# Weights loaded directly behind x, three small rows on GpSimd's queue, the second y ahead of the scores, and adapters gathered two slots earlier

## The chip, the core and the metric

The kernel runs on one core of a Trainium2 chip. A core has five engines with a queue of instructions each: PE (matrix products; its weight loads are shown apart, as PEld), DVE (vector work), ACT (activation functions and copies), POOL (GpSimd) and SP (which here only issues transfers). Transfers between device memory and the core's on-chip memory run on 16 DMA engines that all queues share; SP, ACT and POOL can each issue them. The engines wait for each other through semaphores. What is measured is the device time of one execution in microseconds (us); lower is better.

## What is computed

Eight batches of 128 tokens with 512 features pass through two residual layers. The first adds a product with one of 16 adapter matrices, chosen by an index per batch. The second adds grouped-query attention over a paged cache of 512 old keys plus the 128 new ones. (The cached rows of the eight batches are found through a table of page numbers.)

```python
def _L0_cond_ref(x, adapter_ids, weight):
    w = weight[adapter_ids]
    return jnp.einsum('bsi,boi->bso', x, w)

def _L1_cond_ref(x, Wq, Wk, Wv, Wo, q_norm_w, k_norm_w, k_cache, v_cache, block_table, cache_seqlens):
    q = jnp.einsum('bsd,ed->bse', x, Wq).reshape(bsz, seqlen, HQ, D)
    k = jnp.einsum('bsd,ed->bse', x, Wk).reshape(bsz, seqlen, HK, D)
    v = jnp.einsum('bsd,ed->bse', x, Wv).reshape(bsz, seqlen, HK, D)
    q = _rmsnorm(q, q_norm_w)
    k = _rmsnorm(k, k_norm_w)
    pos = cache_seqlens[:, None] + jnp.arange(seqlen)[None, :]
    q = _rope(q, pos)
    k = _rope(k, pos)
    kc = k_cache[block_table].reshape(bsz, L, HK, D)
    vc = v_cache[block_table].reshape(bsz, L, HK, D)
    k_all = jnp.concatenate([kc, k], axis=1)
    v_all = jnp.concatenate([vc, v], axis=1)
    ...
    scores = jnp.einsum('bqhd,bkhd->bhqk', q, k_all) * SCALE
    scores = jnp.where(valid[:, None, None, :], scores, -1e+30)
    probs = jax.nn.softmax(scores, axis=-1)
    o = jnp.einsum('bhqk,bkhd->bqhd', probs, v_all)
    o = o.reshape(bsz, seqlen, HQ * D)
    return jnp.einsum('bse,de->bsd', o, Wo)

x = x + _L0_cond_ref(x, itok_B_0_15, L0_cond_weight)
x = x + _L1_cond_ref(x, ..., itok_Bx16_0_63, itok_B_207_1644)
```

There are 32 query heads and 8 key heads of 128 features (`HQ`, `HK`, `D`), and all arithmetic is in 32-bit floating point.

## The kernel before

**Steps and slots.** The 8 key heads are cut into 4 groups of 2. A step `i` is one pair of group `g` and batch `b`; there are 32 steps, and the eight batches of group 0 come first (steps 0 to 7). A step has 8 slots, one for each query head `h`. In a slot PE computes one head's scores (`sc`, L1040), DVE adds the mask and finds the row's bound (L1050), ACT takes the exponential (L1066), POOL divides by the sum (L1114) and DVE transposes blocks of the probabilities (L875). The list `main` holds the remaining matrix work of the step: the products with the values of the step before (`o`), the projections of the next step (`pj_kv`, `pj_q`), the output products (`out`). It is dealt out evenly over the slots by estimated cost. The order in which the program is written is the order in which each engine executes it; nothing is rearranged by a scheduler.

**Queues.** SP issues most transfers, among them the store of transposed probabilities (`xp`), their load back in the other layout (`pT`), and the same pair for the queries (`xq`, `qT`) and for the cached keys (`xk`, `kT`). Transfers of one queue are issued in order, and an issue that waits holds back those behind it. ACT issues the loads of x and of the first weights at the start, and weights of later groups. POOL issues the indirect loads (gathers): cached keys (`kc`), cached values (`vc`) and adapters (`lraw`), each about 1 us of POOL's time.

**The start.** `load_x(0)` puts the first x on ACT's queue (L111), then three short rows (L118, called at L120 to L122): the sequence lengths, the page table and the rope frequencies. Then follow the key weights and the value weights, half a megabyte each (`load_first`, L149). SP loads the first adapter, the query weights, x of batch 1, adapter 1, x of batch 2 and the output weights. POOL fills constants, builds the identity, and issues three other rows: the adapters' numbers and the two norm weights. PE then turns (transposes through PSUM, against the identity) everything that is loaded: `warm` is nine such transposes of the identity itself, with no use but to have PE run. `rope_angles` copies the row to floating point on DVE, spreads it over the 128 partitions by a product on PE (`spread(0)`, L386), and computes angles and their reduction to one turn. `row_numbers` and `row_values` compute on POOL the row numbers by which keys and values are gathered; `row_rest` spreads the second part of the row (`spread(1)`), from which come `lora_ix`, the row numbers of the adapters, and the norm weights `wn`. `rope_sin`, `rope_cos` and `rope_table` make the tables SW and CW that the rotation of k and q reads.

**The adapters.** Batches 0 and 1 have their adapters loaded by SP at the start. For the others `gather_lora(b)` issues one indirect load of 1 MB into the only buffer of that kind. `turn_lora` transposes it in four pieces (`lw`), in slots 0 to 3 of step `b - 2` (2 to 5 of step 0), and `lora_y` multiplies x with it (`y`), after which x + y is transposed again (`turn_x1`). In step `i` below 5, `gather_lora(b + 3)` stands in slot 6, behind the scaling of that slot's probabilities and behind two gathers of values.

**The second y.** Just before step 0, one of the four pieces of `lora_y(1)` is emitted; the other three go into `main` of step 0, behind the first scores, and after them output weights and `turn_x1(1)`. Pieces of work that evacuate PSUM stand in a list `pending`, and `run(pending)` emits them.

**Buffers.** PSUM has four buffers of 512 columns (`ps_mm`) for everything but the scores, and two (`ps_sc`) for scores.

Of the kernel before, what the change touches and what calls it, by code (L numbers as in the profile page):

```python
# [18 lines left out]
P = 128  # L19
# [33 lines left out]
def lora_then_paged_attention(  # L53
# [49 lines left out]
    def load_x(b, eng=None):  # L103
        (eng or nc.sync).dma_start(out=acc[b], in_=x[b])
# [12 lines left out]
    def load_row(eng, to, lo, src):  # L117
        eng.dma_start(out=to[:, lo : lo + src.shape[-1]], in_=src)  # L118

    load_row(nc.scalar, row_i, at_len, seqlens.unsqueeze(0))  # L120
    load_row(nc.scalar, row_i, at_bt, block_table.rearrange("b n -> (b n)").unsqueeze(0))
    load_row(nc.scalar, row_f, 0, inv_freq.unsqueeze(0))  # L122


    def weight_rows(kind, g, n, m=1):
# [72 lines left out]
    nc.gpsimd.memset(ones, 1.0)  # L198
    ident = const.tile([P, P], FP, name="ident")
    make_identity(nc, ident)  # L200
    wn = const.tile([P, 2, D], FP, name="wn")
    par = const.tile([P, 1], I32, name="par")
    nc.gpsimd.iota(par, pattern=[[0, 1]], base=0, channel_multiplier=1)
# [171 lines left out]
    def table_set(func):  # L375

        nc.scalar.activation(rope["one"], rope["one"], func)
# [11 lines left out]
    def rope_angles():  # L389
        nc.vector.tensor_copy(row_f[:, at_len:at_ids], row_i[:, at_len:at_ids])  # L390
        row = spread(0)
        nc.vector.tensor_copy(len_f, row[:, at_len:at_bt])
        nc.vector.tensor_copy(
            rows_of["bt_f"].rearrange("p c q -> p (c q)"), row[:, at_bt:at_ids]
        )
        par_f = rope["par"] = const.tile([P, 1], FP, name="par_f")
        nc.vector.tensor_copy(par_f, par)
        pos = const.tile([P, B], FP, name="pos")
        nc.vector.tensor_scalar(pos, len_f, par_f, None, ALU.add)
        def temp(tag):  # L400
            t = work.tile([P, 4, D], FP, tag=tag, name=f"rope_{tag}")
            return t.rearrange("p h (u d) -> p (h u) d", u=2)

        ang, turns, sin, cos = temp("q0"), temp("q1"), temp("tq0"), temp("sw")
        nc.vector.tensor_tensor(
            ang,
            pos.unsqueeze(2).to_broadcast([P, B, H2]),
            row[:, 0:H2].unsqueeze(1).to_broadcast([P, B, H2]),
            ALU.mult,
        )  # L410
        nc.vector.tensor_scalar(turns, ang, 1.0 / (2 * math.pi), ROUND, ALU.mult, ALU.add)
        nc.vector.tensor_scalar(turns, turns, ROUND, None, ALU.subtract)
        for part in (TWO_PI_1, TWO_PI_2, TWO_PI_3):
            nc.vector.scalar_tensor_tensor(
                out=ang, in0=turns, scalar=-part, in1=ang, op0=ALU.mult, op1=ALU.add
            )
        nc.vector.tensor_scalar(ang, ang, PI_BELOW, -PI_BELOW, ALU.min, ALU.max)
        rope.update(ang=ang, sin=sin, cos=cos)

    def row_rest():  # L420

        nc.vector.tensor_copy(row_f[:, at_ids:at_wn], row_i[:, at_ids:at_wn])
        row = spread(1)
        nc.vector.scalar_tensor_tensor(
            out=lora_ix,
            in0=row[:, 0:B],
            scalar=float(HID // 4),
            in1=rope["par"].to_broadcast([P, B]),
            op0=ALU.mult,
            op1=ALU.add,  # L430
        )
        for n in range(2):
            lo = B + (1 - n) * D
            nc.scalar.copy(wn[:, n, :], row[:, lo : lo + D])
# [493 lines left out]

    on_act, on_vec = nc.scalar.copy, nc.vector.tensor_copy

    t = ps_mm.tile([P, HID], FP, tag="mm", name="warm")
    for n in range(9):
        nc.tensor.transpose(t[:, 0:P], ident, ident)
    row_parts()
    table_set(AF.Sin)
    rope_angles()
    row_numbers()
    for c in range(LC):
        gather_k(0, c)
    row_values()  # L940
    turn_x(0, on_act)
    for n in range(4):
        turn_weights(("kv", 0, n), on_act)
    for j in range(4):
        turn_lora_row(0, j, (on_act, on_vec)[j % 2])
    row_rest()
    rope_sin()
    rope_table(1, ("sin",))
    rope_cos()
# [11 lines left out]
        f()  # L961
    rope_table(0)
    make_mask(0)
    run(pending)
    for _, f in project(0, "q0"):
        f()
# [3 lines left out]
    run(pending)  # L970
    for c in range(LC):
        gather_k(1, c)
    row_tables(range(1, G))
    for _, f in project(0, "q1"):
        f()
    turn_x(1, on_vec)
    for c in range(KC):
        turn_lora(1, c, on_vec if c % 2 else on_act, True)
    gather_lora(2)
    turn_k(0, 0, on_act)  # L980
    turn_q(0, 0, on_act)
    turn_x(2, on_vec)
    y_1 = lora_y(1)
    y_1.pop(0)[1]()
    for _ in range(3):
        load_next()

# [2 lines left out]
    for i, (g, b) in enumerate(steps):  # L990
        s = st[i]
        main = []
        if i == 0:
            main += y_1

            def second(n):
                run(pending)
                turn_weights(("o0", 0, n))
                if n == 2:
                    turn_x1(1)  # L1000

            main += [(4 * TR * (1 + n // 2), lambda n=n: second(n)) for n in range(3)]
            main += [(4 * TR, lambda: turn_weights(("o0", 0, 3)))]
        early = i >= B - 2
        if i and not early:
            main += values(i - 1, 0)
# [22 lines left out]
        for h in range(8):  # L1029
# [98 lines left out]
                    pending.append(lambda i=i: make_mask(i + 1))  # L1128
            if g == 0 and h == 6 and b + 3 < B:
                load_x(b + 3)  # L1130
                gather_lora(b + 3)
            if 8 * i + h - 1 in turn_when:
                load_next()
# [58 lines left out]
```

## Time and profile before

| What | Value |
|---|---|
| Time before, median of 3 runs | 1201.35 us (1200.62 to 1202.08) |
| The profiled execution, its own time | 1202.72 us |
| Its span, first to last instruction | 1201.0 us |
| PE busy | 1183.7 us (99%) |
| DVE busy | 733.3 us (61%) |
| POOL busy | 673.3 us (56%) |
| ACT busy | 530.4 us (44%) |
| Bytes moved | 328.04 MB, mean 273 GB/s |

The span is what the profile's instructions cover; the 1.7 us between it and the execution's own time lie around it. Times in the profile's views count from the start of the span. In a line of a timeline the first number is the start, the second the duration, then engine, line of the code, operation, what is written and read, shapes, and a count; in square brackets stands how long the engine was idle before it, and what ended that. An engine's name with a q is its queue: it issued a transfer there. "Landing" is when a transfer's semaphore says that all has arrived.

A busy share of 99% does not say that PE runs at its full pace: matmuls are pipelined, their ends are modelled, and the same instruction takes twice as long when PE's clock is halved.

### The profile page before, as it was taken

The numbers are of one execution on the slowest core, as the hardware profiler recorded it, in microseconds if no ns is written. First come the engines' busy times: TensorE is split into PE (matmuls) and PEld (weight loads), VectorE is DVE, ScalarE is ACT, GpSimd is POOL, SyncE is SP. The second block draws the span as 40 slices with busy tenths as digits, with TensorE's granted clock in tenths as the row PEclk, the third lists the DMA queues.
The fourth block names the chain that finished last, engine by engine and source line by source line (L and its number), as shares of the span: only waits on it lengthen the run. The fifth ranks groups of instructions, "written<-read, shape, count | busy, mean of one in ns | idle before, by whom it ended". The sixth has DMA issues, their size and how long they took to land.

```text
span 1201.0 us, 12981 instructions
## 1 busy us (share of the span) xinstructions
PE 1183.7 (99%) x3421; PEld 580.3 (48%) x3421; DVE 733.3 (61%) x1676; ACT 530.4 (44%) x1647; POOL 673.3 (56%) x780
## 2 busy tenths in 40 slices
PE   7999999999999999999999999999999999999998
PEld 5555444454444444444444444444444444444454
DVE  5575655656566667666566666666557655565651
ACT  4564444444444444444444444444444444444432
POOL 4466456445565556656655556565555656655540
PEclk9999999999999999999999999999999999999999
DMA  8288788778989989888898998888898987777761
GB/s 289 96 276 270 262 297 275 238 258 259 312 288 301 341 296 305 295 281 291 291 297 287 334 326 285 309 268 305 268 317 282 297 290 257 249 251 247 257 221 60
DMA packets 187120, 328.04 MB, mean 273 GB/s; under 512 B 13094, under 2 KB 106023, under 8 KB 178087
## 3 DMA queue, kind: packets, MB, share of 16 engines
q1 hardware_dynamic: 124000, 238.71, 58.9%
q10 hardware_dynamic: 49798, 48.64, 12.4%
q0 software_dynamic: 13248, 39.86, 10.1%
q8 instruction: 28, 0.46, 0.2%
q14 instruction: 46, 0.37, 0.1%
HBM read 195.04 MB, written 132.12 MB: 272 GB/s over the span
## 4 chain that ended last, share of the span: by engine, by line
PE 90%; DMA 3%; POOL 3%; issue 1%; DVE 1%; ACT 1%; ACTq 0%; POOLq 0%; DVEq 0%
PE sc L1040 22%; PE o L563 21%; PE pj_q L563 17%; PE out L563 16%; PE pj_kv L563 9%; DMA lraw<-in_L_cond_weight_dram,lora_ix 2%; PE y L563 2%; PE lw L478 1%; DMA raw_kv<-in_L_cond_Wv_dram 1%; DMA w_q<-xw_q 1%; POOL kc L614 1%; PE kt L767 1%; POOL p L1114 1%; POOL vc L614 1%; POOL rs L691 0%
## 5 line engine op out<-in xcount | busy, mean ns | idle before, releaser
L1050 DVE CUSTOM_DVE_ANT_0 p<-sc,mask 128x640 f32<-128x640 f32 x256 | 210.9, 824 | 403.4 <-PE sc L1040 403.1
L1066 ACT ACTIVATE p<-p,mn 128x640 f32<-128x640 f32 x256 | 211.6, 827 | 313.9 <-DVE mn L1050 310.2
L1040 PE MATMUL sc<-kT,qT 128*128 128x512 f32 (+1 forms) x1024 | 319.4, 434 | 0.2 <-ACT qT L777 0.2
L1114 POOL TENSOR_SCALAR p<-p,rc 128x640 f32<-128x640 f32 x252 | 201.9, 801 | 186.0 <-DVE rc L1107 184.1
L1040 PEld LDWEIGHTS sc<-kT,qT 128*128 128x128 f32 x1024 | 190.6, 191 | 226.8 <-issue 206.9
L563 PE MATMUL pj_q<-w_q,x1T 128*128 128x512 f32 x512 | 236.1, 593 | 0.3 <-DMA w_q<-xw_q 0.2
L563 PE MATMUL out<-w_o,oT 128*128 128x512 f32 (+1 forms) x528 | 235.0, 580 | 0.9 <-ACT oT L842 0.7
L563 PE MATMUL o<-pT,vc 128*128 128x512 f32 x512 | 235.4, 592 | 0.0
L875 DVE STREAM_TRANSPOSE tp<-p 128x640 f32<-128x640 f32 x252 | 211.0, 837 | 5.7 <-POOL p L1114 5.4
L614 POOL DMA_INDIRECT kc<-in_L_cond_k_cache_dram,key_ix x128 | 131.2, 1025 | 31.8 <-issue 31.5
L614 POOL DMA_INDIRECT vc<-in_L_cond_v_cache_dram,val_ix x128 | 127.9, 999 | 30.5 <-issue 30.3
L696 ACT ACTIVATE q<-q,rs 128x128 f32<-128x128 f32 x256 | 81.9, 390 | 132.5 <-POOL q L683 124.7
L563 PEld LDWEIGHTS out<-w_o,oT 128*128 128x128 f32 x528 | 95.4, 190 | 91.6 <-issue 88.9
L563 PEld LDWEIGHTS pj_q<-w_q,x1T 128*128 128x128 f32 x512 | 92.7, 190 | 94.4 <-issue 92.5
L563 PEld LDWEIGHTS o<-pT,vc 128*128 128x128 f32 x512 | 92.5, 190 | 92.3 <-issue 86.3
L563 PE MATMUL pj_kv<-w_kv,x1T 128*128 128x512 f32 x256 | 116.6, 593 | 0.7 <-ACT x1T L480 0.7
L675 POOL TENSOR_TENSOR k<-sw 128x256 f32<-128x256 f32 x31 | 23.0, 741 | 160.1 <-PE kt L767 139.4
L683 POOL TENSOR_TENSOR q<-q,sw 128x512 f32<-128x512 f32 x59 | 74.4, 1262 | 44.1 <-DVE sw L666 44.0
L650 ACT ACTIVATE sq<-pj_q 128x128 f32<-128x128 f32 x256 | 70.8, 277 | 59.5 <-PE pj_q L563 50.5
L691 POOL TENSOR_TENSOR rs<-ss,mhalf 128x6 f32<-128x6 f32 x64 | 77.1, 1205 | 5.3
L563 PEld LDWEIGHTS pj_kv<-w_kv,x1T 128*128 128x128 f32 x256 | 46.0, 190 | 45.5 <-issue 44.6
L563 PE MATMUL o<-pT,vn 128*128 128x512 f32 x128 | 65.7, 595 | 0.0
(124 smaller groups left out, 879.6 us busy)
## 6 DMA issues: line engine op xcount, KB each, us to landing
xp<-tp SPq DMA_DIRECT2D x63, 1280.0 KB, 6.0
pT<-xp SPq DMA_DIRECT2D x63, 1280.0 KB, 6.6
xk<-tk SPq DMA_DIRECT2D x31, 512.0 KB, 7.6
kT<-xk SPq DMA_DIRECT2D x62, 256.0 KB, 6.5
xq<-tq SPq DMA_DIRECT2D x59, 256.0 KB, 3.8
qT<-xq SPq DMA_DIRECT2D x59, 256.0 KB, 6.0
st_q<-in_L_cond_Wq_dram ACTq DMA_DIRECT2D x24, 256.0 KB, 5.3
xw_q<-tw_q ACTq DMA_DIRECT2D x24, 256.0 KB, 4.6
```

What stands on the lines that cost most here:

```text
L563: nc.tensor.matmul(y[0], lhsT=lhsT, rhs=rhs, start=(k == 0), stop=(k == len(pieces) - 1))
L614: nc.gpsimd.indirect_dma_start(out=dst[:, c, :], out_offset=None, in_=src, in_offset=bass.IndirectOffsetOnAxis(ap=rows[:, g, at : at + 1], ...
L650: nc.scalar.activation(sq, t[:, h, :], AF.Square, scale=float(D) ** -0.5, accum_out=ss[:, h : h + 1])
L675: nc.gpsimd.tensor_tensor(dst.rearrange("p h (i a) -> p h a i", a=4), cw.rearrange("p h (a i) -> p h a i", a=4), sw[:, 0:heads, :].rearran ...
L683: add.tensor_tensor(dst, cw, sw[:, 0:heads, :], ALU.add)
L691: nc.gpsimd.tensor_tensor(rs[:, 0:width], ss[:, 0:width], mhalf[:, 0:width], ALU.pow)
L696: nc.scalar.activation(q, q, AF.Identity, scale=rs[:, h : h + 1])
L875: nc.vector.transpose(u.tp[:, :, r, :], u.p.pop(r).rearrange("q (a k) -> q a k", a=4))
L1040: nc.tensor.matmul(sc[:, lo:hi], lhsT=s.qT[j][:, r, :, :].rearrange("d h q -> d (h q)"), rhs=s.kT[j].rearrange("d a c i -> d (a c i)")[:, ...
L1050: nc.vector.tensor_tensor_reduce(out=p, in0=sc[:, 0:LA], in1=masks[i % 2].rearrange("p a c i -> p (a c i)"), scale=1.0, scalar=3.0e38, op0 ...
L1066: nc.scalar.activation(p, p, AF.Exp, bias=unit.mn[:, one], scale=-1.0, accum_out=unit.sm[:, one])
L1114: nc.gpsimd.tensor_scalar(q, p, unit.rc[:, one], 1.0, ALU.mult, ALU.mult)
```

## The change

Four things move, and nothing is computed differently.

- The three short rows of ACT's queue are issued on POOL's queue instead, right behind the identity. So on ACT's queue the key and value weights follow x directly.
- The order of the start changes: ten warming transposes; then x's transposes and the first two of the key/value weights; then `rope_angles`, without the reduction; then the other two; and eight more warming transposes before the first adapter's. The cast of the adapters' numbers moves ahead of the copies of the first adapter, and the reduction of the angles (`rope_rest`, three operations and a clamp) behind `row_rest`. The six small table operations (`row_tables`) move ahead of k's first rotation.
- The second y, all four pieces, and its addition go ahead of the third x's transposes and of the first scores, and `gather_lora(2)` behind them. Step 0 then starts with `turn_x1(1)` and the four output weights.
- `gather_lora(b + 3)` stands in slot 4 in steps 1 to 4, still in slot 6 in step 0.

```diff
-    load_row(nc.scalar, row_i, at_len, seqlens.unsqueeze(0))
-    load_row(nc.scalar, row_i, at_bt, block_table.rearrange("b n -> (b n)").unsqueeze(0))
-    load_row(nc.scalar, row_f, 0, inv_freq.unsqueeze(0))
...
     make_identity(nc, ident)
+    load_row(nc.gpsimd, row_i, at_len, seqlens.unsqueeze(0))
+    load_row(nc.gpsimd, row_i, at_bt, block_table.rearrange("b n -> (b n)").unsqueeze(0))
+    load_row(nc.gpsimd, row_f, 0, inv_freq.unsqueeze(0))
...
         nc.vector.tensor_scalar(turns, turns, ROUND, None, ALU.subtract)
+        rope.update(ang=ang, turns=turns, sin=sin, cos=cos)
+        nc.vector.tensor_copy(row_f[:, at_ids:at_wn], row_i[:, at_ids:at_wn])
+
+    def rope_rest():
+        ang, turns = rope["ang"], rope["turns"]
         for part in (TWO_PI_1, TWO_PI_2, TWO_PI_3):
...
         nc.vector.tensor_scalar(ang, ang, PI_BELOW, -PI_BELOW, ALU.min, ALU.max)
-        rope.update(ang=ang, sin=sin, cos=cos)
 
     def row_rest():
 
-        nc.vector.tensor_copy(row_f[:, at_ids:at_wn], row_i[:, at_ids:at_wn])
         row = spread(1)
...
-    t = ps_mm.tile([P, HID], FP, tag="mm", name="warm")
-    for n in range(9):
-        nc.tensor.transpose(t[:, 0:P], ident, ident)
+    def warm(n):
+        t = ps_mm.tile([P, HID], FP, tag="mm", name="warm")
+        for _ in range(n):
+            nc.tensor.transpose(t[:, 0:P], ident, ident)
+
+    warm(10)
     row_parts()
     table_set(AF.Sin)
+    turn_x(0, on_act)
+    for n in range(2):
+        turn_weights(("kv", 0, n), on_act)
     rope_angles()
+    for n in range(2, 4):
+        turn_weights(("kv", 0, n), on_act)
     row_numbers()
     for c in range(LC):
         gather_k(0, c)
     row_values()
-    turn_x(0, on_act)
-    for n in range(4):
-        turn_weights(("kv", 0, n), on_act)
+    warm(8)
     for j in range(4):
         turn_lora_row(0, j, (on_act, on_vec)[j % 2])
     row_rest()
+    rope_rest()
     rope_sin()
...
     make_mask(0)
+    row_tables(range(1, G))
     run(pending)
...
-    row_tables(range(1, G))
     for _, f in project(0, "q1"):
         f()
     turn_x(1, on_vec)
     for c in range(KC):
         turn_lora(1, c, on_vec if c % 2 else on_act, True)
-    gather_lora(2)
     turn_k(0, 0, on_act)
     turn_q(0, 0, on_act)
+    for _, f in lora_y(1):
+        f()
+    run(pending)
     turn_x(2, on_vec)
-    y_1 = lora_y(1)
-    y_1.pop(0)[1]()
+    gather_lora(2)
...
         if i == 0:
-            main += y_1
-
-            def second(n):
-                run(pending)
-                turn_weights(("o0", 0, n))
-                if n == 2:
-                    turn_x1(1)
-
-            main += [(4 * TR * (1 + n // 2), lambda n=n: second(n)) for n in range(3)]
-            main += [(4 * TR, lambda: turn_weights(("o0", 0, 3)))]
+            main += [(4 * TR, lambda: turn_x1(1))]
+            main += [(4 * TR, lambda n=n: turn_weights(("o0", 0, n))) for n in range(4)]
...
             if g == 0 and h == 6 and b + 3 < B:
                 load_x(b + 3)
+            if g == 0 and h == (4 if i else 6) and b + 3 < B:
                 gather_lora(b + 3)
```

## The prediction

> **What bounds the kernel now.** I read the chain of waits first, then the list of what the matmul engine (PE) waited for, then the start and the adapter stalls in time, and last the DMA shares.
>
> The chain's share by line, from the page:
>
> ```profile
> PE 90%; DMA 3%; POOL 3%; issue 1%; DVE 1%; ACT 1%; ACTq 0%; POOLq 0%; DVEq 0%
> ```
>
> PE sets the end; its 1183.7 us of work hardly changes here. A change can only take away what is left, 17.3 us in which PE stands still, and stretches in which it runs slowly. The waits of PE over the whole run (total us, times, longest):
>
> ```profile
> PE wt_kv L496 <- DMA raw_kv<-in_L_cond_Wv_dram: 4.1, 1, 4.1
> PE lw L478 <- DMA lraw<-in_L_cond_weight_dram,lora_ix: 3.3, 3, 2.2
> ...
> PE spread L386 <- issue: 0.9, 1, 0.9
> ...
> PE x L478 <- DVE acc L588: 0.7, 1, 0.7
> PE pj_kv L563 <- ACT x1T L480: 0.7, 1, 0.7
> ```
>
> Each part of the change aims at one of these: the value weights, the adapters, and the pair around the second y. The start, in time:
>
> ```profile
> 1.16 0.53 ACTq L118 DMA_DIRECT2D row_i<-in_itok_B_dram  x1
> ...
> 2.25 0.75 POOL L118 DMA_DIRECT2D row_i<-in_itok_B_dram  x1
> 2.29 0.40 ACTq L149 DMA_DIRECT2D raw_kv<-in_L_cond_Wk_dram  x1
> ...
> 2.72 0.49 ACTq L149 DMA_DIRECT2D raw_kv<-in_L_cond_Wv_dram  x1
> ...
> 11.74 1.94 PE L496 MATMUL wt_kv<-ident,raw_kv 128*128 128x128 f32 x8 [4.07 <-DMA raw_kv<-in_L_cond_Wv_dram]
> ```
>
> The value weights are asked for at 2.72 and used at 11.74. The DMA view of the first 16 us gives, as its last column, the time from issue to landing of rows that GpSimd's queue carries:
>
> ```profile
> raw_kv<-in_L_cond_Wv_dram ACTq DMA_DIRECT2D x1, 512.0 KB, 8.9
> ...
> row_i<-in_itok_B_dram POOLq DMA_DIRECT2D x1, 0.0 KB, 4.2
> row_f<-in_L_cond_k_norm_w_dram POOLq DMA_DIRECT2D x1, 0.5 KB, 6.5
> row_f<-in_L_cond_q_norm_w_dram POOLq DMA_DIRECT2D x1, 0.5 KB, 7.2
> ```
>
> The longest adapter stall (PE in time), and the window of 3.4 us behind it (its last three columns are PE's clock, DMA share, GB/s):
>
> ```profile
> 202.11 3.60 PE L563 MATMUL o<-pT,vc 128*128 128x512 f32 x8
> 207.93 1.03 PE L478 MATMUL lw<-ident,lraw 128*128 128x128 f32 x4 [2.22 <-DMA lraw<-in_L_cond_weight_dram,lora_ix]
> 208.76 2.34 PE L1040 MATMUL sc<-kT,qT 128*128 128x512 f32 x4
> ```
>
> ```profile
> 208.00:211.40 3.40, 3.40 (x9) 2.18 (x10) 0.27 (x1) 0.59 (x1) 0.00 (x0) 0.50 1.00 386
> ```
>
> The stall costs twice: PE waits, and then runs 3.4 us at clock 0.50.
>
> **Part C, the adapters.** For steps 1 to 4 the gather moves on GpSimd's queue from behind two value gathers of slot 6 to behind the scaling of slot 4, about 12 us earlier (step 2: 159.04 to 146.9, where POOL is idle 2.59 us until 149.43). The issue itself, 0.95 us, fits in that gap, so the key gathers at 150.39 do not move. A load takes 5.6 to 8.2 us to land, so it lands by 156 where 163.9 is needed. From start to start eight out or o matmuls take 3.44: lw was due at 163.90, 205.55 and 250.32 and came at 164.83, 207.93 and 250.78, so 0.93 + 2.38 + 0.46 = 3.77 us go. The clock: from lw to the next pj_kv it is 164.83 to 167.24 = 2.41 us at full clock, 207.93 to 212.01 = 4.08 us here; 1.67 us more go. Together 5.4.
>
> The megabyte now meets other traffic. Two lines of windows, slots 4 to 7 of steps 1 and 2:
>
> ```profile
> 106.00:118.00 12.00, 12.00 (x36) 5.87 (x35) 5.98 (x15) 3.91 (x15) 8.14 (x10) 1.00 0.91 291
> ```
> ```profile
> 147.00:159.00 12.00, 12.00 (x36) 5.75 (x35) 7.97 (x17) 6.44 (x21) 8.21 (x9) 1.00 0.95 316
> ```
>
> At 400 GB/s, the best of the first 16 us, 1 MB takes all DMA engines 2.6 us; free are 9% of 12 = 1.1 us and 5% = 0.6 us. What is late next is q transposed for the next step's first scores, queued on SP's queue behind a load of probabilities. It was issued at 109.58, 151.41 and 237.61 and landed 7.4, 5.8 and 5.6 us later; the scores began at 118.25, 158.94 and 245.37. Margins 1.2, 1.8, 2.2 us; delays 2.6 less what is free, 1.5, 2.0, 1.4. Waits 0.3, 0.2, 0; for step 3 (no landing in the records, 7% free) I put 0.2. Sum 0.7. Bounds: 0 if all is absorbed, and, with 2.6 unabsorbed at each, 1.4 + 0.8 + 0.8 + 0.4 = 3.4. I take 0.7, since the free share is measured. C: 4.7 (2.0 to 5.4).
>
> [...]
>
> **Part A, the start.** Three row loads leave ACT's queue, so key and value weights go out 1.1 us earlier (1.16 and about 1.6). The rows now stand on POOL's queue from 1.44, right behind the identity; with the row issues' own 0.75, 0.56 and 0.50 the third goes out at 2.75, and the iotas and the other three rows, the memsets and ACT's first activation behind them move back 1.8 us (covered: selections are needed only once the rows are there, the norm rows at 13.0 at worst, before their product). In PE's order the spread of the rows now stands between the two halves of the weights' transposes, so these wait for the later of two things. First, the value weights: 6.3 at best (1.6 + 3.4 like the key weights + 1.3 for 0.5 MB at 400 GB/s), 10.5 at worst (1.6 + 8.9). Second, the rows: landing at 2.75 + 4.2 = 6.95 to 2.75 + 7.2 = 9.95, then 1.23 for the cast and the product (3.49 to 4.72 before): 8.2 to 11.2. The row issued at 2.25 took 4.2 us, that at 3.01 took 6.5; I put 5.2 for 2.75, so the second half starts at 9.2 instead of 11.74: 2.5 earlier (0.5 to 3.5).
>
> From there to y it was 6.8 us. Added: eight warming transposes at 0.24 (1.94 over 8), 1.9. Removed: 0.9 of PE's wait for the cast of the identifiers, which now precedes; and part of the half-speed transposes (sixteen took 3.57 at 13.47, 2.03 at 22.08): 0 to 1.7, I take 0.9. That is even; the one more at the very start ends before x has landed.
>
> Against it stands the angle reduction, three operations of 0.72 and one of 0.43 on DVE, moved behind the second spread. It was hidden under the 4.07 wait; now sine waits for it, 2.3 us later than before against y, then the tables, then y's addition 1.5 later. PE covers with sixteen transposes of the query weights, but the fourth needs y's PSUM buffer, and ACT's eight copies of 0.5 stand behind the cosine: pj_kv starts 9.0 after the spread instead of 7.5. Cost 1.5 (at least 1.0). The key gathers (landed at 21.2, needed at 33.0) and the table rows, which fill a DVE gap of 1.3 before k's rotation with 0.7, cost nothing. A: 1.0 gained (-1.0 to 2.5).
>
> [...]
>
> **Part B, the second y.** From the third x's transposes (41.39) to pj_kv (51.40) PE has 8.24 us of work in 10.01. In the new order y runs 41.4 to 44.8, x 45.3, scores 46.4; DVE does q's rotation first (to 45.9), then y's addition to 47.0, so x1's transposes wait 0.6. ACT copies x1T only behind the first exponential, at 49.5 to 50.0; the last output weights wait for that buffer, 1.3 more. The second scores then end at 51.6: 0.2 lost (at best 1.8 gained, no wait at all; at worst 1.0 lost, one more exponential and copy). The first softmax is 3.6 us late; behind it wait the value gathers, with 16 us to spare (60.8 to 77.0). The second adapter's gather goes from 41.97 to 45.4 and lands by 53.6; it is needed at 56.7, so 3 us cover it.
>
> **Sum.** 1.0 - 0.2 + 4.7 = 5.5 us. The profiled execution took 1202.72 (span 1201.0 and 1.7 around it): 1197.2. It lies 1.4 above the median 1201.35; if the others lack the slow clock, they gain 3.8: 1197.5. I forecast 1197.3.
>
> **Rivals.**
> 1. Only the adapters pay: rows land 7.2 us after issue, A is -1.0; 4.7 - 1.0 - 0.2 = 3.5, or 1.8 from the median: 1199.4. For it: the norm rows took 6.5 and 7.2. Against: the new rows leave before them.
> 2. All goes well: A 2.5, B 0.5, C 5.4: 8.4, so 1194.3. For it: DMA has gaps in steps 1 to 4. Against: the margin of 1.2 us.
> 3. Slower: the megabyte holds the probabilities' store, then, because their load waits for it, that load and q behind it, so 2 x 2.6 less 1.0 free: 4.2, less a margin of 1.75, 2.4 at four step heads, 9.8. C becomes -4.4: with A and B 1202.72 + 3.6 = 1206.3. It decides above (5.4 + 0.8) / 4 = 1.6 us per head. For it: shares of 0.91 and 0.95. Against: in step 2 the store had landed at 148.8, when the gather's data would only begin.
> That the gather does not move is excluded by the order of instructions.
>
> **Chances.** Forecast 0.52, rival 1 0.23, rival 2 0.17, rival 3 0.08. Within 0.2% (2.4 us, about what a measurement here can tell) means 1198.9 to 1203.8: rival 1 mostly. Faster 0.73, same 0.18, slower 0.09. The forecast's own range is 1195 to 1199; with most of the rivals 1 and 2, 1193.6 to 1200.8.
>
> **What would show it.** No wait of lw for lraw in steps 2 to 5 and no stretch of clock 0.50; Wv's transposes at about 9.2, ended by the rows and not by Wv; pj_kv of batch 0 near 25 instead of 26.13; first scores of steps 2 to 5 waiting under 0.4 us for q. I am wrong if these scores wait over 1.6 us, or if Wv's transposes start after 11.

## The result, and the profile after

The changed kernel took 1203.34 us (median of 20 runs, 1201.55 to 1208.33) beside 1201.40 us of the kernel before (20 runs, 1199.05 to 1203.70): a ratio of 1.0021, 95% interval 1.0011 to 1.0030. By the ratio it is slower by some 2.5 us (the medians differ by 1.9), where 4 us less had been forecast. Its profiled execution took 1203.91 us with a span of 1202.1 us. All lines of "after" below are from that execution.

The chain of waits of the changed kernel, by engine:

```profile
PE 87%; DMA 7%; DVE 2%; ACT 1%; POOL 1%; issue 1%; ACTq 0%; SPq 0%; DVEq 0%; POOLq 0%
```

The share of DMA in the chain went from 3% to 7%, and PE's fell from 90% to 87%. The list of what PE waited for (total us, times, longest) says where:

```profile
PE sc L1043 <- DMA qT<-xq: 3.9, 3, 2.1
PE spread L386 <- DMA row_f<-in_inv_freq_dram: 1.7, 1, 1.7
...
PE wt_kv L499 <- DVE rope_q L405: 1.0, 1, 1.0
PE sc L1043 <- ACT qT L780: 0.9, 1, 0.9
PE wt_q L499 <- DVE acc L591: 0.9, 1, 0.9
PE wt_o L499 <- ACT x1T L483: 0.8, 1, 0.8
PE o L566 <- DMA pT<-xp: 0.8, 2, 0.5
```

Two lines of before are gone: that of `lw` for `lraw`, 3.3 us in three, and that of `wt_kv` for the value weights, 4.1 us. At the top stands a new one: the first scores of steps 3, 4 and 5 wait 3.9 us for q. The waits moved to a place five microseconds earlier in the step instead of going away. At the start, 1.7 and 1.0 us stand in place of the 4.1. The chain through the longest of the new waits (start, us, what):

```profile
146.49 0.68 DVE tq L814
147.17 0.02 issue
147.19 6.67 DMA xq<-tq
153.86 0.02 issue
153.88 5.97 DMA qT<-xq
159.85 0.14 issue
159.98 1.85 PE sc L1043 x4
```

Read it upwards. The scores start when the load of qT is down (159.85). That load was issued when the store of xq was down (153.86), and that store of 256 KB took 6.67 us. In the kernel before, the same store was issued 30.08 us after the step's first score, here 30.11, so nothing on the engines made it later. There it took 3.08 us, from its issue to that of the load. SP's queue in the kernel before:

```profile
148.33 0.32 SPq L813 DMA_DIRECT2D xq<-tq  x1
...
151.41 0.37 SPq L820 DMA_DIRECT2D qT<-xq  x1
```

The load took 5.97 us, 5.8 before. The lost time is in the store. A slow store need not reach the head, though: in step 1 it took 6.8 us instead of 3.5, but the load behind it was down within 5.4 us instead of 7.4, and the head of step 2 did not wait.

The half clock came back too. Two windows of the changed kernel (start:end, us, then busy times of PE, PEld, DVE, ACT, POOL; the last three columns are PE's clock, the DMA share and GB/s):

```profile
157.90:159.98 2.08, 0.03 (x1) 0.03 (x1) 0.00 (x0) 0.00 (x0) 1.60 (x3) 1.00 1.10 350
160.63:164.04 3.41, 3.41 (x10) 2.01 (x9) 2.17 (x5) 1.32 (x3) 0.22 (x1) 0.50 0.30 101
```

PE is idle for 2.05 us, and from 160.63 on it runs 3.41 us at half clock, as it did from 208.00 on, behind the stall of 2.22 us for the adapters, in the kernel before.

The heads of the steps (first scores), after minus before, in us: step 1 -1.2, step 2 -1.2, step 3 +1.0, step 4 +2.8, step 5 0.0, step 6 -0.4, step 9 -0.5, step 11 +0.8, and about the same to the end. So the start and the first step were 1.2 us ahead; heads 3 and 4 gave back 4.0; the step in which before had its longest stall returned 2.8; and steps 9 and 10 lost another 1.4, through short waits for `pT` and for output weights.

### The profile page after: what moved, and what is told of

Its sections match the earlier page's. It is cut to its first block, busy times and chain, and to the rows that moved or that the text cites. A ratio compares the mean times of both kernels' runs of the same rounds, so it can differ in the third digit from the quotient of the medians.

```text
span 1202.1 us, 13003 instructions
## 1 busy us (share of the span) xinstructions
PE 1184.1 (99%) x3430; PEld 580.0 (48%) x3430; DVE 734.4 (61%) x1676; ACT 529.6 (44%) x1647; POOL 675.5 (56%) x783
## 4 chain that ended last, share of the span: by engine, by line
PE 87%; DMA 7%; DVE 2%; ACT 1%; POOL 1%; issue 1%; ACTq 0%; SPq 0%; DVEq 0%; POOLq 0%
PE o L566 21%; PE sc L1043 21%; PE pj_q L566 16%; PE out L566 16%; PE pj_kv L566 9%; DMA xq<-tq 2%; DMA qT<-xq 1%; DMA pT<-xp 1%; PE lw L481 1%; PE y L566 1%; DMA w_o<-xw_o 1%; DMA w_q<-xw_q 1%; PE kt L770 1%; DMA xp<-tp 0%; DMA row_f<-in_inv_freq_dram 0%
## 5 line engine op out<-in xcount | busy, mean ns | idle before, releaser
L686 POOL TENSOR_TENSOR q<-q,sw 128x512 f32<-128x512 f32 x59 | 74.6, 1265 | 43.0 <-DVE sw L669 42.8
```

The costliest lines, as they stand in the source:

```text
L686: add.tensor_tensor(dst, cw, sw[:, 0:heads, :], ALU.add)
```

## The experiments

The time of each kernel is compared with the kernel before, run beside it on the same chip, as a ratio with its 95% interval; in us it is the ratio's distance from 1 times 1201.4.

| Kernel | Ratio (interval) | us | PE's waits for `lraw` | for `qT` loaded |
|---|---|---|---|---|
| changed kernel | 1.0021 (1.0011 to 1.0030) | +2.5 | none | 3.9 in 3 |
| slot 4 alone | 1.0018 (1.0007 to 1.0029) | +2.2 | none | 4.6 in 3 |
| start and second y, slot 6 | 0.9991 (0.9978 to 1.0004) | -1.1 | 5.5 in 3 | none |
| changed, slot 3 | 1.0051 (1.0033 to 1.0069) | +6.1 | none | 6.1 in 4 |
| start alone | 0.9992 (0.9981 to 1.0002) | -1.0 | 3.3 in 2 | none |
| second y alone | 1.0001 (0.9991 to 1.0011) | +0.1 | 4.9 in 2 | none |
| changed, front of slot 3 | 1.0004 (0.9995 to 1.0013) | +0.5 | none | 4.2 in 3 |
| changed, half the rows | 0.9985 (0.9975 to 0.9995) | -1.8 | 0.2 | 1.7 in 2 |
| changed, no rows | 0.9966 (0.9952 to 0.9980) | -4.1 | none | none |
| changed, front of slot 6 | 0.9960 (0.9944 to 0.9975) | -4.8 | 0.2 | none |
| changed, q ahead of p | 1.0121 (1.0096 to 1.0145) | +14.5 | none | 0.2 |
| front of slot 6 alone | 0.9967 (0.9953 to 0.9981) | -4.0 | 0.2 | none |
| start and front of slot 6 | 0.9963 (0.9950 to 0.9977) | -4.4 | none | none |

The theory from the two traces: the gather's megabyte takes the DMA engines from the store of xq, so q is late at the heads. The first four runs take the change apart and move the gather.

### 1. Slot 4 alone

```diff
 (kernel before)
             if g == 0 and h == 6 and b + 3 < B:
                 load_x(b + 3)
+            if g == 0 and h == (4 if i else 6) and b + 3 < B:
                 gather_lora(b + 3)
```

> The kernel before with one thing changed: adapters gathered in slot 4 of the steps after the first, start and second y as before. Theory (the gather's 1 MB in large packets slows the store of xq that runs beside it, so the load of qT is issued late and the heads of steps 3, 4 and 5 wait for it): the 3.8 us of waits for lraw are gone, and in their place the first score of steps 3 to 5 waits 2 to 5 us in all for qT, with or without one stretch of clock 0.50 (1.7 us); time within -2.5 to +2.5 us of before. Rival R1 (slot 4 is harmless by itself, and the new order of the start and of the first step makes the heads late): no wait for qT above 0.3 us at any head, time 4 to 5.5 us below before. Rival R2 (the loss lies in the steps after the eighth, not at the heads): heads 3 to 5 without waits, later steps longer by over 1 us.

Measured: 1203.92 us, 2.2 us above before. The waits of PE, and the chain at the head of step 3:

```profile
PE sc L1040 <- DMA qT<-xq: 4.6, 3, 2.3
```

```profile
148.01 6.32 DMA xq<-tq
154.33 0.02 issue
154.35 6.09 DMA qT<-xq
160.44 0.14 issue
160.57 1.32 PE sc L1040 x4
```

With the old start and the old second y, the same store is slow (6.32 us) and the same heads wait. The place of the gather alone makes the kernel slower: R1 falls. R2 is not clean: this profile too loses some 1.5 us in later steps (15, 17 and 18), but the 4.6 us of waits are at the heads.

### 2. The change without slot 4

```diff
 (changed kernel)
-            if g == 0 and h == (4 if i else 6) and b + 3 < B:
+            if g == 0 and h == 6 and b + 3 < B:
                 gather_lora(b + 3)
```

> The changed kernel with the gather of the adapters put back to slot 6; the new start and the second y ahead of the scores stay. Theory: nothing at the heads of steps 3 to 5 waits for qT above 0.3 us, the waits for lraw come back as before (3 to 4.5 us), and what is left is the gain at the head of step 1, 1.2 us: 0.8 to 2.2 us below before. Rival R1 (the new order makes the heads late): waits for qT at heads 3 to 5 of 3 us or more, time 1 to 4 us above before. Rival R2 (steps 9 and 10 lose 1.4 us through the new order): those two steps 35.1 us or longer again, time -0.5 to +1 us of before.

Measured: 1.1 us below before, an interval from 2.6 below to 0.5 above. No head waits for a load of q. The adapters' wait is back, and larger than expected:

```profile
PE lw L481 <- DMA lraw<-in_L_cond_weight_dram,lora_ix: 5.5, 3, 2.8
```

Steps 9 and 10 have their normal 34.62 us, so the new order doesn't cause the loss there by itself. Rivals R1 and R2 fall.

### 3. Slot 3, the first idea for a repair

The DMA view of the changed kernel showed a quiet stretch ahead of the store (share 0.37 from 138 to 143 us), so the gather was put there.

```diff
 (changed kernel)
-            if g == 0 and h == (4 if i else 6) and b + 3 < B:
+            if g == 0 and h == (3 if i else 6) and b + 3 < B:
                 gather_lora(b + 3)
```

> The changed kernel with the gather in slot 3 instead of 4, some 5 us earlier, right behind the last use of the adapters before. Theory (it hurts only because its packets meet the store of xq): the megabyte is down when the store is issued, the store takes about 3 us again, no head waits above 0.3 us for qT, no wait for lraw, no half clock between 20 and 1190 us: 5 to 7 us below before. Rival R3 (a megabyte anywhere in the step makes qT late, or slot 3 collides with the store all the same because the gather is slow by itself): waits at the heads of 2 us or more remain, time -2 to +2 us of before. Rival R4 (the earlier gather waits on its buffer and holds the instructions behind it on its engine): POOL waits some us at the gather and the masks or k rows behind it come late.

Measured: 6.1 us above before, more than 11 us from what was expected. From the chain at the head of step 3:

```profile
143.38 0.94 POOL lraw L240
144.33 0.07 issue
144.40 0.20 POOL ss L693
144.60 0.08 issue
144.68 1.37 POOL rs L694
...
151.04 4.84 DMA xq<-tq
155.88 0.02 issue
155.90 7.66 DMA qT<-xq
```

Two things went wrong. The issue of the gather is itself on the chain: POOL's `ss` and `rs`, on which the new q and k wait, stand behind it, so the store goes out 31.6 us after the step's first score instead of 30.1. And the rows moved only from 145 to 150, so the packets of the store of the probabilities, 1.28 MB on SP's queue, ran from 148 to 153, where they had run from 143 to 148 in the kernel before (this step began 1.2 us later). It now ran beside the store of xq; and the load of pT, which must wait for it (issued 34.8 us into the step, against 30.6 in the kernel before), went out right in front of the load of qT, which took 7.66 us. R4 holds in part. R3 holds for the waits, though its time, within 2 us of before, was missed too: the theory's "it hurts only because its packets meet the store of xq" was too narrow.

### 4. The start alone

The edit is the changed kernel's start (the first and second item of the section on the change), on the kernel before.

> The kernel before with the new start alone (rows on GpSimd's queue, key and value weights directly behind x); second y and gather as before. Theory: the key and value projection starts 0.9 us earlier and this stays to the head of step 1; heads 3 to 5 as before: 0.4 to 1.5 us below before. Rival R1 (the new order of the start by itself makes something late in step 0 or at heads 3 to 5): the gain of 0.9 us is gone by the head of step 5, time 0 to 2 us above before.

Measured: 1.0 us below before, an interval from 2.3 below to 0.2 above. In this profile the key and value projection begins at 24.97 instead of 26.13. That looks like the gain of 0.9 that was expected; the other runs below say what it is.

### 5. The second y alone

```diff
 (kernel before)
-    gather_lora(2)
     turn_k(0, 0, on_act)
     turn_q(0, 0, on_act)
+    for _, f in lora_y(1):
+        f()
+    run(pending)
     turn_x(2, on_vec)
-    y_1 = lora_y(1)
-    y_1.pop(0)[1]()
+    gather_lora(2)
... (and the list of step 0, as in the change)
```

> The kernel before with the second y ahead of the scores alone (with it the gather for batch 2 stands behind the turning of x of batch 2); start and slot 6 as before. Theory: the projection of key and value of batch 1 starts 0.8 us earlier, of which 0.7 us are given to a longer wait for qT at the head of step 1; the time is 0 to 1 us below before. Rival R5 (it is this part that makes the whole change slower): head of step 2 over 0.5 us later than in the kernel before, time 0.5 to 2 us above.

Measured: 0.1 us above before, 1.1 below to 1.3 above. From the first projection to the head of step 1 it is 49.60 us (24.70 to 74.30), against 49.29 in the kernel before: 0.3 lost. With the new start under both it is 48.82 without this part (start alone) and 49.01 with it (changed kernel): 0.2 lost. R5 falls.

### 6. The front of slot 3

```diff
 (changed kernel)
+            if g == 0 and i and h == 3 and b + 3 < B:
+                gather_lora(b + 3)
             if i < last:
                 if i + 1 < last and h in ((3, 5) if i else (4, 5)):
                     ...
-            if g == 0 and h == (4 if i else 6) and b + 3 < B:
+            if i == 0 and h == 6 and b + 3 < B:
                 gather_lora(b + 3)
```

> The changed kernel with the gather in slot 3, ahead of the gathers of keys there and so some 4 us earlier than in the run with slot 3, where the rows moved from 2 us behind the issue and pushed the next transfers back. Theory T2 (the DMA engines have one quiet stretch of 5 us in a step, and 1 MB costs the head what of it lies outside): the rows move in the quiet stretch, the store of xq takes 3 to 4 us again, GpSimd's issue costs the chain ahead of the store 1.3 us, of which 1.6 us of slack hide most; waits for qT at heads 3 to 5 of 0 to 1 us each, 2 to 6 us below before. Rival R3 (a megabyte costs the head its 2.6 us wherever it stands in the step): waits of 2 us or more at the heads, time 0 to 5 us above before.

Measured: 0.5 us above before, waits of 4.2 us in three, as R3 had it: T2 missed. The chain at the head of step 3:

```profile
148.99 3.17 DMA xq<-tq
152.16 0.02 issue
152.18 8.22 DMA qT<-xq
160.39 0.14 issue
160.53 1.79 PE sc L1043 x2
```

The store of xq is quick again (3.17), as T2 said, and the head is as late as in the changed kernel. The store of the probabilities took from 142.45 to the issue of the load of pT at 150.19, 7.7 us (5.8 before: 143.03 to 148.83), so that load, 1.28 MB on the same queue right ahead of the load of qT, came 1.9 us later in the step; qT behind it took 8.22 us. All of this belongs to one line of transfers that ends at the head; whichever of them the megabyte is put in front of, the last one is late.

### 7 and 8. Half the rows, and none

```diff
 (changed kernel; half the rows)
-    def gather_lora(b):
-        lraw[b] = lora_tile(b)
+    def gather_lora(b, n=P):
+        lraw[b] = lora_tile(b) if n == P else lraw[b - 1]
         nc.gpsimd.indirect_dma_start(
-            out=lraw[b],
+            out=lraw[b][0:n, :],
...
-                gather_lora(b + 3)
+                gather_lora(b + 3, P // 2 if i else P)
```

```diff
 (changed kernel; no rows)
-            if g == 0 and h == (4 if i else 6) and b + 3 < B:
+            if i == 0 and h == 6:
                 gather_lora(b + 3)
+            if g == 0 and i and h == 4 and b + 3 < B:
+                lraw[b + 3] = lraw[b + 2]
```

> The changed kernel, gather in slot 4, but of 64 rows instead of 128 from step 1 on; the other half of the adapters is left as it was, so this leaves out half of the transfer. Theory (what delays the store of xq is the time that the rows take on the DMA engines): the store takes 4.5 to 5 us, between 3.1 without a gather and 6.5 with the whole; waits for qT at heads 3 to 5 of 0 to 0.7 us each, time 3 to 6 us below before. Rival R6 (not the bytes but GpSimd's issue and the slow first packets do it): store 6 us or more, waits as with the whole gather, time within 1 us of the changed kernel's.

> The changed kernel without the gathers of the steps after the first, so this leaves out three transfers of 1 MB (the adapters of the later batches are those of batch 3). It is the bound for every place of the gather. Theory: no wait for lraw, none for qT above 0.3 us at heads 3 to 5, no half clock there; 5 to 7 us below before. Rival R1 (the order of the first steps makes qT late): waits for qT at heads 3 to 5 remain, of 1 us or more each. Rival R2 (the later steps lose): steps 9 and 10 are 35 us or longer again.

(The transfers left out are four, those of steps 1 to 4.) Measured: 1.8 and 4.1 us below before. The profiled spans, 1197.0 and 1195.8 us, are 4.0 and 5.2 below; the medians show less than expected. Without rows no head waits for a load of q; with half of them:

```profile
PE sc L1043 <- DMA qT<-xq: 1.7, 2, 1.3
```

The store of xq, from its issue to that of the load, in steps 2, 3 and 4: without rows 3.1, 2.9 and 3.7 us, with half of them 5.7, 5.0 and 6.6, with all 6.7, 5.6 and 7.3. So the gather is the cause, and R1, R2 and R6 (no gain with half) fall. But half the bytes cost the store 2.6 us on average and all of them 3.3: not in proportion, which the theory had expected; R6's slow first packets come back in what follows. The DMA view of the changed kernel, 147 to 154 us, in 40 slices of 0.175 us:

```profile
DMA  9999999904891745986979959999996989999998
GB/s 316 348 369 389 398 415 568 196 23 70 117 246 59 164 140 211 281 304 246 573 257 351 433 222 398 433 456 375 410 398 260 486 357 366 392 363 418 413 497 328
...
q0 software_dynamic: 166, 1.13, 55.9%
q1 hardware_dynamic: 707, 0.88, 34.8%
```

And that of the run without rows, the same 7 us:

```profile
GB/s 351 0 15 120 278 366 336 363 454 360 395 392 375 410 386 290 170 140 272 287 319 336 366 263 336 366 278 307 322 424 336 278 307 190 278 263 322 410 442 392
...
q1 hardware_dynamic: 1192, 1.84, 85.1%
```

The queue lines give packets, MB, and the time of the packets as a share of 16 engines. SP's transfers are q1: in these 7 us they moved 0.88 MB beside the gather and 1.84 MB without it. The gather (q0, with some keys) moved 1.13 MB and held 55.9% of the engines for 7 us, 3.9 us of all of them. With half of the rows the same line reads:

```profile
q0 software_dynamic: 80, 0.52, 40.7%
```

That is less than half of the bytes and almost three quarters of the engines' time. And the rate falls when the gather's packets begin: from 148.2 to 149.8 (slices 8 to 16) the mean is 136 GB/s, against 381 in the same slices without it. In this step little moves while the gather starts. That this makes half of the rows so dear is not shown: in step 1 of the changed kernel 351 GB/s moved in the first 1.6 us of the gather (106.39 to 107.99), and the store was as late (6.8 us with all of the rows, 6.4 with half, 3.5 without).

### 9. The front of slot 6

If everything up to the head is one line, the megabyte has to stand behind the load of qT, and in time for `lw`, 5 us after the head. In slot 6 two gathers of values stood ahead of it. They are needed a step later.

```diff
 (changed kernel)
+                if g == 0 and h == 6 and b + 3 < B:
+                    gather_lora(b + 3)
                 for c in {6: (0, 1), 7: (2, 3)}.get(h, ()) if i else (range(LC) if h == 7 else ()):
                     gather_v(i + 1, c)
...
-            if g == 0 and h == (4 if i else 6) and b + 3 < B:
-                gather_lora(b + 3)
```

> The changed kernel with the gather in slot 6, as before, but ahead of the two gathers of values there: 2.7 us earlier than in the kernel before, 10 us later than in the changed kernel. Theory (the megabyte costs the head only what moves between the store of the probabilities and the load of qT; behind that it has the 5 us until the turns of the adapters): the load of qT is down before the rows start, no head waits above 0.3 us for qT; the rows land 2.7 us earlier than before, so that of the waits for lraw (3.3 us in three) 0 to 1 us is left and the clock stays at 1.0 from step 1 on; 3.5 to 6.5 us below before. Rival R3 (a megabyte costs its 2.6 us wherever it stands): waits of 1 us or more in two or more steps, for qT or for lraw, time within 2 us of before.

Measured: 1196.49 us, 4.8 us below before (3.0 to 6.7), the lowest ratio of all. POOL in time, and what was left of the waits:

```profile
155.12 0.79 POOL L1117 TENSOR_SCALAR p<-p,rc 128x640 f32<-128x640 f32 x1
156.09 1.11 POOL L240 DMA_INDIRECT lraw<-in_L_cond_weight_dram,lora_ix  x1 [0.18 <-issue]
157.51 0.96 POOL L617 DMA_INDIRECT vc<-in_L_cond_v_cache_dram,val_ix  x1 [0.30 <-issue]
158.77 0.94 POOL L617 DMA_INDIRECT vc<-in_L_cond_v_cache_dram,val_ix  x1 [0.30 <-issue]
```

```profile
PE lw L481 <- DMA lraw<-in_L_cond_weight_dram,lora_ix: 0.2, 1, 0.2
```

The store of xq takes 3.1 us, the load of qT lands at 157.88 (needed at 158.53), the rows at 162.76 (needed at 163.6). From 20 us on no wait of PE is longer than 0.9 us, and the mean granted clock of the whole span is 0.997. As good as without rows at all, within the intervals: what the gather cost can no longer be seen. R3, a fixed price wherever it stands, falls.

### 10. The load of q ahead of the load of p

```diff
 (changed kernel)
+                    late = int(i > 0 and g == 0 and u.j == 0)
-                    to_read.append((8 * i + h, 1, lambda u=u: receive(u)))
+                    to_read.append((8 * i + h + late, 1, lambda u=u: receive(u)))
...
-            to_read[:] = [r for r in to_read if r[0] == 8 * i + h]
+            to_read[:] = [r for r in to_read if r[0] >= 8 * i + h]
```

> The changed kernel, gather in slot 4 as there, but on SyncE's queue the load of qT (256 KB) stands ahead of the load of the turned probabilities pT (1.28 MB) of the same slot in the first steps, where it stood behind it. Theory T3 (the head is late because the gather, the store of xq and the load of pT all have to pass before qT): the waits at heads 3 to 5 fall from 3.9 us to 0 to 1 us in all, the product o behind the head now waits for pT, 0 to 1 us in each step, and no half clock comes; 2 to 5 us below the changed kernel. Rival R7 (the store of xq is what is late, the load of pT in front of qT costs nothing): waits for qT stay at 3 us or more in all, time within 1 us of the changed kernel.

Measured: 14.5 us above before. Neither theory had this. PE's longest wait, and the chain at it:

```profile
PE x L481 <- DMA acc<-in_x_dram: 13.1, 4, 5.5
```

```profile
152.73 5.76 DMA xq<-tq
...
158.98 0.45 SPq L905
159.43 0.05 issue
159.48 7.42 DMA acc<-in_x_dram
```

The wait for qT is gone (0.2 us), as T3 said. But the load of x (`acc`), which stood behind both, now has the whole 1.28 MB of pT in front of it at the latest moment: pT is issued at 158.98, because the queue stands until the store of xq is down, and in the changed kernel it had gone out at about the time of the store's issue (147.63 beside 147.19). One thing is clean here: with no load of pT beside it, the store of xq behind a gather in slot 4 still took 5.76 us (3.1 without rows). So it is the gather that slows it, not the load of pT.

### 11 and 12. The front of slot 6 on the kernel before, and with the start

The edits are that of run 9 on the kernel before, and on the start alone.

> The kernel before with nothing changed but the place of the gather: slot 6, ahead of the gathers of values. Theory: waits for lraw 0 to 1 us instead of 3.3, no wait for qT, no half clock: 2.5 to 5 us below before. Rival R3: within 1 us of before.

> The kernel before with the new start and the gather in slot 6 ahead of the gathers of values; second y as before. Theory (the parts add up, and the second y is worth nothing): 3.5 to 6.5 us below before, within 1 us of the run that has the second y too.

Measured: 4.0 us (2.3 to 5.6) and 4.4 us (2.8 to 6.0) below before. With the start and the second y it was 4.8. The three intervals lie on each other: the place of the gather brings nearly all, and what start and second y add can't be told from nothing.

### The line of transfers, by run

Us after the first score of step 2; a step without waits is 40.69 us long, so q is needed at 40.55. The column "Store" is from the store's issue to that of the load that waits for it; landings are from the chain or the transfers' records.

| Kernel | Gather issued | Store xq issued | Store | qT down |
|---|---|---|---|---|
| before | 40.8 | 30.1 | 3.1 | 38.9 |
| front of slot 6 | 38.1 | 30.1 | 3.1 | 39.9 |
| changed (slot 4) | 28.8 | 30.1 | 6.7 | 42.8 |
| slot 4 alone | 28.8 | 30.1 | 6.3 | 42.5 |
| half the rows, slot 4 | 28.8 | 30.1 | 5.7 | 42.0 |
| slot 3 | 24.0 | 31.6 | 4.9 | 44.1 |
| front of slot 3 | 21.1 | 31.3 | 3.2 | 42.7 |

With the gather issued at 21.1, 24.0 and 28.8, q is down 1.5 to 3.6 us too late; at 38.1 and 40.8 it is in time.

## Why the prediction was wrong, point by point

**What failed: the term of the new waits in part C.** The prediction laid 2.6 us of transfer, less a free share, on the *load* of q, against margins of 1.2 to 2.2 us, and got 0.7 us in all. Measured are 3.9 us of waits, more than the upper bound of 3.4, and one stretch of half clock at these heads (160.63 to 164.04), for which nothing was put. The prediction's own sign of being wrong, scores that wait over 1.6 us for q, was there at step 3 (2.05). Two things in that step were wrong:

- The transfer in the way was missed. The gather, put at 146.9, was to be followed within two microseconds by the store of xq (148.33 in the profile of before; in the one after 145.86 and 147.19). The delay was laid on the load, and the store that it waits for was left out, though the trace of before shows it, with 3.08 us. In step 2 the store took 3.1 us without rows, 5.7 with half and 6.7 with all of them (run 8, run 7 and the changed kernel).
- The price of the megabyte was too low. 2.6 us is 1 MB at 400 GB/s; the gather, with some keys, held the DMA engines for 3.9 us, and in its first 1.6 little moved (136 GB/s in all). The free share, 5% to 9%, was counted as a relief; the store alone lost 3.3 us on average, more than the 2.6 without any relief.

**The removed waits of part C: right.** The adapters' wait is gone in every run with the gather in slots 3 and 4 (0.2 at most). Its size in the profile of before, 3.3 us, is at the low end of the four profiles with slot 6 as before (3.3 to 5.5). Run 11, which takes this wait away and puts no other in its place, gains 4.0 us (2.3 to 5.6); 5.4 had been put. The 1.67 us of half clock went and came back at another stall: behind 2.05 us of idle the clock was 0.50 from 160.63 to 164.04.

**Part A, 1.0 us: not shown.** In the two profiles the key and value projection came 0.94 us earlier, at 25.19 instead of 26.13, as put. The transposes of the value weights began at 9.36 (9.2 put), ended by the rows and not by the weights. The start of the changed kernel, PE in time:

```profile
8.86 0.57 PE L386 MATMUL spread<-row_f,pages 1*128 1x200 f32 x2 [1.72 <-DMA row_f<-in_inv_freq_dram]
9.36 0.66 PE L499 MATMUL wt_kv<-ident,raw_kv 128*128 128x128 f32 x4
11.06 1.09 PE L499 MATMUL wt_kv<-ident,raw_kv 128*128 128x128 f32 x4 [1.03 <-DVE rope_q L405]
```

But over all profiles the projection begins at 24.97 to 26.99 with the new start (ten kernels, mean 25.97) and at 24.70 to 26.13 with the old one (four, mean 25.47). What varies is how fast PE runs at the start (the sixteen transposes of the first adapter took 2.02 us in the changed kernel, 2.27, 2.28 and 2.68 in runs 3, 4 and 2, 3.57 in the kernel before), and with the new start also when the rows land: PE waits 1.5 to 3.1 us for them. The two profiles were one draw from each, and that they agreed with the forecast was luck. The start alone measured 1.0 us below before, but its interval reaches to 0.2 above, and with the front of slot 6 the start moved the median from 1197.45 to 1197.73. The wait of 1.03 us for DVE's `rope_q` wasn't in the list of steps; most of it was made up by the first adapter's transposes, which in this profile took 2.02 us instead of 3.57, with the clock at 1.00 from 13.85 on (0.9 had been counted on). The means put the part at -0.5, the median of the start alone at 1.0; no run here decides between them. Of the ten profiles with the new start only that of run 6 has a wait of PE for the value weights, 0.4 us.

**Part B, -0.2 us: right.** Runs 4 and 5 show 0.2 to 0.3 lost by the head of step 1; the wait of `wt_o` for x1T is there (0.8 us), shorter than the 1.3 put, and in its place the head of step 1 waits 0.9 us for ACT's copy of q.

**The rivals.** The third, "slower", was nearest in mechanism: a megabyte that holds a store, then a load, then q, and decides above 1.6 us per head. It named the store of the probabilities and four heads at 2.4 us. In the changed kernel it is q's own store, at three heads, 2.05, 0.84 and 1.02; with the gather in slot 3 it is also the one that was named. The argument against it ("the store had landed at 148.8, when the gather's data would only begin") was true of the wrong store.

**The sum.** Put: 1.0 - 0.2 + 4.7 = 5.5 us gained. Measured: the start 1.0 (-0.2 to 2.3), the second y -0.1, slot 4 alone -2.2 (-0.8 to -3.5), together -1.3; the whole, -2.5 (-1.3 to -3.6). Within their intervals the parts add up, and the error is that of part C.

**What stays open.** The waits at the heads in place of those of the adapters explain some 1 us of the 2.2 (4.6 against 3.3, with a mean granted clock of 0.999 in both profiles). Steps behind the sixth lose 1.0 to 1.5 us in some profiles, by waits for `pT` or for turned weights: the changed kernel 1.4, slot 4 alone 1.5, slot 3 1.0, but also the start alone (1.2) and the start with the front of slot 6 (1.1). With one profile for each kernel it can't be said whether a slot has a part in that, and it wasn't tried.

## What to carry to other kernels

Before a transfer is moved earlier, list every transfer that is issued between its new place and the deadline next behind it, in the order of issue, stores that loads wait for among them; one line of transfers ends at that deadline, and extra bytes in it can make its last one late: here they did in steps 2 to 4 from each of the three places tried (3.9 to 6.1 us of waits), and in step 1 from one of them. To bring a late load forward, look first at what stands directly ahead of it in its own queue with a later need: here two issues, 2.7 us, were all that was wanted, and 12 us were too much. A difference of about 1 us that two profiles show in a stage with a varying clock has to be seen in more than two.

## What the runs showed of the hardware

**Half clock came behind some stalls of 2 us and more, and not behind others.** In the kernel before, the granted clock was 0.50 from 208.00 to 211.41, behind a stall of 2.22 us that ended at 207.93; in the changed kernel from 160.63 to 164.04, behind one of 2.05 us that ended at 159.98, and at the start from 10.44 to 13.85. Each of the three lasted 3.41 us. In the timelines of the kernel before, the changed kernel and runs 2 to 6, `lw` and the heads have nine stalls above 2 us. Behind six of them (the 2.22 and 2.05 above, 2.78 and 3.14 in runs 2 and 3, 2.33 and 2.01 in runs 5 and 6) work ran slowly: four transposes of `lw` took 1.03 to 1.04 us where 0.60 to 0.63 is normal, four matmuls of a head 1.85 to 2.34 where it is 1.24 to 1.32, and in run 3 the eight of `o` 5.02 instead of 3.60. Behind the other three (2.50, 2.13 and 2.58 in runs 2, 4 and 5), and behind one of 2.47 us in run 10, it did not, nor behind shorter ones of 1.81, 1.59, 1.29, 1.19 and 1.02 us (runs 1, 3, 7 and 4, and the changed kernel). So the length of a stall alone does not tell these apart: 2.01 us had slow work behind it, 2.58 had not. What decides is not shown.

**The gather's price was not in proportion to its bytes.** In step 2 of the changed kernel, in the 1.6 us in which the gather's first packets ran, all queues together moved 136 GB/s; the run without it moved 381 in the same place. Counted from the gather's first packet, the first 1.6 us moved 351, 171, 243 and 210 GB/s in steps 1 to 4, the rest of the gather 360 to 391. Half of the rows cost the store of xq more than three quarters of what all of them do (2.6 of 3.3 us); whether the low rate at the start has a part in that is open.
